# First MLP product by Strassen's seven products, gathered in PSUM; the blocks of both MLP matrices by turns in one buffer

## The chip, the cores and the metric

The kernel runs on one core of a Trainium2 chip. The metric is the device time in microseconds (us) of one execution; lower is better. TensorE multiplies matrices into PSUM, VectorE and ScalarE do elementwise work and read PSUM, GpSimd (POOL) does small elementwise work in SBUF, and SyncE (SP) mostly issues DMA transfers. Each engine works through its own queue in order; between engines there are semaphores.

## The reference

All data are fp32. x is (16, 256, 32, 32): 16 images of 256 channels and S = 1024 pixels. Two layers follow one another:

```python
# layer 0: attention, 4 heads of 64, over the 1024 pixels of an image
qkv = xs @ w_proj + b_proj
res = softmax(q k^T * 64**-0.5) v
x   = res @ w_out + b_out + xs

# layer 1
x = x + attention(group_norm(x), qkv_w, proj_w, proj_b, phys_bias)   # 8 heads of 32
h = group_norm(x)                                                  # 32 groups
h = einsum('oc,bchw->bohw', mlp_w1, h) + mlp_b1                    # 256 -> 1024
h = gelu(h)                                                        # the exact form
h = einsum('oc,bchw->bohw', mlp_w2, h) + mlp_b2                    # 1024 -> 256
return x + h
```

## The kernel before

An image lies in SBUF as 128 partitions x 2 channel blocks x 1024 pixels; the pixels are handled in two blocks of TB = 512. `first_pass` goes through the images in one Python loop, fully unrolled (L1001). Iteration b consists of

- attention 0 of image b (`attention_a`, L354): 32 steps, one for each of 4 (pixel block, channel block) items and 8 blocks of keys. A step makes the scores (L368), their exponential `e` on ScalarE (L376, 8 buffers), the weighing (L389) two steps behind, and on VectorE the running sum of the exponentials `es` (L401), from which the denominators `den` come;
- the first MLP product of image b-1 (`hidden`, L846), 16 pieces, run after attention 0 by `run_pieces` (L1017). In iteration 0 the q, k, v products of image 1 stand here;
- attention 1 of image b (`attention_b`, L478), whose gaps are filled with q, k, v products of the next image's attention 0 and the second MLP product of image b-1 (`reduce`, L886).

Image 15's MLP comes after the loop with no attention beside it (L1066).

**Later work.** `Later` (L31) holds functions with a number of ticks; a tick follows each step of an attention and each piece. The end of attention 0 runs through it beside the MLP pieces: `denominators` (L327) copies the denominators out (L328), spreads them over all partitions by DMA (L333), takes the reciprocal (L337), sends it back through a DRAM row (L338, L343), and `scale` (L440) multiplies the result with it (L446). Four ticks later the projection `out_proj` (L630) runs: products into the two single PSUM banks, then `leave` (L639) adds to x (L641) and takes statistics (L644). The group norm (L668) follows: `means`, three ticks later `variances` (a product `gm` with a 128x128 averaging matrix, then four tiny VectorE operations), one tick later `apply` (a product `gv`, an inverse square root on POOL, the normalised tile by L723). The last denominators of attention 1 are handled in the same way across the border to the next image: they are spread before, and inverted (L337) three steps into attention 0 of the next.

**Order.** A scheduler orders the instructions of each engine by readiness in its own model of the times, so the order need not be the program's. `keep_in_program_order` pins an instruction behind the one traced before it on its engine; the reciprocal L337 and the scaling L446 are pinned so.

**PSUM.** Eight banks of 128 x 512 fp32: three pairs (`wide`, L267), given out with the longest unused first, and two single banks (`bank`).

**The MLP before.** `hidden` makes one 128 x 512 block of the 1024 x 1024 hidden values: two products of 128x128 weights (L849; one for each channel block) into one PSUM bank, then Gelu with bias by ScalarE (L857) to an SBUF tile `g`. The second matrix is multiplied by Strassen's scheme: its seven 4-block sums of quarters lie in `w2s` (made once by POOL, L150), and VectorE makes the sums of the hidden blocks in place by `combine` (L863, L866). w1 lies whole in SBUF as `w1`. Both are loaded once by SP's queue (L164).

Of the kernel before, what the change touches and what calls it, by code (L numbers as in the profile page):

```python
# [8 lines left out]
F32 = mybir.dt.float32  # L9
I32 = mybir.dt.int32  # L10
AF = mybir.ActivationFunctionType
# [3 lines left out]
P = 128  # L15
# [4 lines left out]
TB = 512  # L20
# [34 lines left out]
def kernel(  # L55
# [21 lines left out]
    nc = tc.nc  # L77
    B, C, S = x.shape
    HID = mlp_w1T.shape[1]
    CC = C // P  # L80
# [51 lines left out]
    wo = load_mat(w_out, "wo")  # L132
    wq = load_mat(qkv_wT, "wq")
    wpj = load_mat(proj_wT, "wpj")
    w1 = load_mat(mlp_w1T, "w1")

    w2s = const.tile([P, 7, HID // P // 2, P], F32, name="w2s")

    def quarter(co, half):
        n = HID // P // 2
        return mlp_w2T.rearrange("(c p) n -> p c n", p=P)[
            :, half * n : (half + 1) * n, co * P : (co + 1) * P
        ]

    for n, q in ((2, (0, 0)), (3, (1, 1)), (4, (0, 1)), (1, (1, 0))):
        weights.append((w2s[:, n], quarter(*q)))

    def sum_quarters():  # L150
        q11, q22 = w2s[:, 2], w2s[:, 3]
        nc.gpsimd.tensor_sub(w2s[:, 5], w2s[:, 1], q11)
        nc.gpsimd.tensor_add(w2s[:, 1], w2s[:, 1], q22)
        nc.gpsimd.tensor_sub(w2s[:, 6], w2s[:, 4], q22)
        nc.gpsimd.tensor_add(w2s[:, 4], w2s[:, 4], q11)
        nc.gpsimd.tensor_add(w2s[:, 0], q11, q22)
        nc.gpsimd.tensor_add(m2b2, m2b, m2b)

    def load_rest():
# [48 lines left out]
    with ExitStack() as first:  # L210
        first_pass(
            first, tc, x, out,
            dict(
                wp=wp, bqk=bqk, pb=pb, bo=bo, g1w=g1w, g1b=g1b, g2w=g2w,
                g2b=g2b, pjb=pjb, m1b=m1b, m2b=m2b, wo=wo, wq=wq, wpj=wpj, w1=w1,
                w2s=w2s, m2b2=m2b2, gavg=gavg, mhalf=mhalf, ones=ones, eones=eones,
                bvo=bvo, at_start=at_start, load_rest=load_rest, exp_bias=exp_bias,
                sum_quarters=sum_quarters,
                in_range=in_range,
            ),  # L220
        )

    good = nc.values_load(in_range[0:1, 0:1], min_val=0, max_val=1)
    with tc.If(good == 0):
        with ExitStack() as again:
            general_pass(
                again, tc, x, out,
                dict(
                    wp=wp, bqk=bqk, pb=pb, bo=bo, g1w=g1w, g1b=g1b, g2w=g2w,
                    g2b=g2b, pjb=pjb, m1b=m1b, m2b=m2b, wo=wo, wq=wq, wpj=wpj, w1=w1,  # L230
                    mlp_w2T=mlp_w2T, gavg=gavg, mhalf=mhalf, b_proj=b_proj,
                ),
            )


def first_pass(ctx, tc, x, out, k):
    nc = tc.nc
    B, C, S = x.shape
    CC, SB, NT = C // P, S // P, S // TB
    HC = k["w1"].shape[2] // P  # L240
    later = Later()

    act = ctx.enter_context(tc.tile_pool(name="act", bufs=1))
# [9 lines left out]
    dram = ctx.enter_context(  # L253
        tc.tile_pool(name="dram", bufs=4, space=bass.MemoryType.DRAM)
    )

# [95 lines left out]
    def attention_a(b, qT, kT, v, project):  # L354
# [85 lines left out]
        def scale(t, full):  # L440
            r = res[:, :, t * TB : (t + 1) * TB]
            halves = [
                y.rearrange(form, c=CC, h=2)
                for y, form in ((r, "p c (h q) -> p c h q"), (full, "p (h c q) -> p c h q"))
            ]
            tc.keep_in_program_order(nc.vector.tensor_mul(halves[0], *halves))  # L446
            if t == NT - 1:
                later.after(4, lambda: project(t, res)())

        cols[0] = 32  # L450
        pending = []
# [213 lines left out]
        return issue  # L665


    def group_norm(key, src, stats, gw, gb, tag, out_tile, wait):  # L668
        st = {}

        def averages(name, src):
            ps = wide(name)
            if cols[0] == P:
                product(ps[:, 0, :CC], k["gavg"], src, start=True, stop=True)
                return [(slice(0, P), ps[:, 0, :CC])]
            halves = [slice(h, h + HALF) for h in range(0, P, HALF)]
            for n, sl in enumerate(halves):
                nc.tensor.matmul(  # L680
                    ps[sl, n, :CC], k["gavg"][sl, sl], src[sl], start=True, stop=True
                )
            return [(sl, ps[sl, n, :CC]) for n, sl in enumerate(halves)]
# [23 lines left out]
        def apply():  # L707
            rstd = small.tile([P, CC], F32, tag="rstd", name=f"rstd_{key}")
            for sl, ps in averages(f"gv_{key}", st["tv"]):
                nc.vector.tensor_scalar(rstd[sl], ps, EPS, None, ALU.add)  # L710
            nc.gpsimd.tensor_tensor(rstd, rstd, k["mhalf"], ALU.pow)
            a = small.tile([P, CC], F32, tag="ga", name=f"ga_{key}")
            nc.vector.tensor_mul(a, rstd, gw)
            ma = small.tile([P, CC], F32, tag="gma", name=f"gma_{key}")
            nc.vector.tensor_mul(ma, st["mean"], a)
            c = small.tile([P, CC], F32, tag="gc", name=f"gc_{key}")
            nc.vector.tensor_sub(c, gb, ma)
            y = act.tile([P, CC, S], F32, tag=tag, name=f"gn_{key}")
            out_tile.append(y)
            for t in range(NT):  # L720
                sl = slice(t * TB, (t + 1) * TB)
                for cc in range(CC):
                    nc.vector.tensor_scalar(  # L723
                        y[:, cc, sl], src[:, cc, sl],
                        a[:, cc : cc + 1], c[:, cc : cc + 1], ALU.mult, ALU.add,
                    )

        means()

# [108 lines left out]

    def mlp(b, xb, hn):
        n4 = HC // 2
        gs = {}

        def hidden(t, hc):  # L846
            ps = wide(f"m1_{b}_{t}_{hc}")[:, 0, :]
            for cc in range(CC):
                nc.tensor.matmul(  # L849
                    ps,  # L850
                    k["w1"][:, cc, hc * P : (hc + 1) * P],
                    hn[0][:, cc, t * TB : (t + 1) * TB],
                    start=(cc == 0),
                    stop=(cc == CC - 1),
                )
            g = work.tile([P, TB], F32, tag="g", name=f"g_{b}_{t}_{hc}", bufs=16)
            nc.scalar.activation(g, ps, AF.Gelu, bias=k["m1b"][:, hc : hc + 1])  # L857
            gs[hc // n4, t, hc % n4] = g
            if hc >= n4:

                combine(*(((0, 1), (1, 1)) if t else ((1, 0), (0, 0))), False, hc - n4)

        def combine(to, what, plus, only=None):  # L863
            for i in range(n4) if only is None else (only,):
# [21 lines left out]
        def reduce(number, right, outs, then):  # L886
            ps = wide(f"m2_{b}_{number}")[:, 0, :]
            for i in range(n4):
                product(
                    ps, k["w2s"][:, number - 1, i], gs[(*right, i)],  # L890
                    start=(i == 0), stop=(i == n4 - 1),
                )
            bias, num = None, 1
# [40 lines left out]
            else:  # L934
                add_up()

        return (
            [lambda t=t, hc=hc: hidden(t, hc) for t in range(NT) for hc in range(HC)],
            [lambda what=what: reduce(*what) for what in products],
        )  # L940


    def run(stage, fill=None):
# [35 lines left out]
        start[1]()  # L979
    run_pieces(start[2:])  # L980
    k["exp_bias"]()
    k["sum_quarters"]()


    def fold_bias():
# [15 lines left out]
    for b in range(B):  # L1001
        if b + 1 < B:
            xs[b + 1] = load_x(b + 1)
        xn = []
        run(
            attention_0(
                b, tiles0, xs[b],
                lambda st, b=b, xn=xn: group_norm(
                    f"g{b}", xs[b], st, k["g1w"], k["g1b"], "res", xn, 3
                ),  # L1010
            )
        )
# [3 lines left out]
            first = first_qk + first_v  # L1016
        run_pieces(first if b == 0 else hidden)  # L1017
        later.flush()
        tiles1, (qk, v) = qkv_1(b, xn[0])
        n = len(qk) // CC  # L1020

# [28 lines left out]
        for m, pieces in enumerate(rest):  # L1050
# [4 lines left out]
                b, tiles1, xs[b],  # L1055
                lambda st, b=b, hn=hn: group_norm(
                    f"h{b}", xs[b], st, k["g2w"], k["g2b"], "q1", hn,
                    3 if b + 1 < B else 1,
                ),
            ),  # L1060
            fill,
        )
        run_pieces(end)
        hidden, outputs = mlp(b, xs[b], hn)
    later.flush()
    run_pieces(hidden + outputs)  # L1066

# [15 lines left out]
def general_pass(ctx, tc, x, out, k):  # L1083
# [1 line left out]
    nc = tc.nc  # L1085
    B, C, S = x.shape
    CC, SB, NT, QT = C // P, S // P, S // TB, TB // P
    HC = k["w1"].shape[2] // P

    act = ctx.enter_context(tc.tile_pool(name="g_act", bufs=1))  # L1090
    work = ctx.enter_context(tc.tile_pool(name="g_work", bufs=2))
# [11 lines left out]
    )  # L1103
    ident = small.tile([P, P], F32, name="g_ident", bufs=1)
    make_identity(nc, ident)
    w2 = act.tile([P, HC, C], F32, tag="w2", name="g_w2")
    nc.gpsimd.dma_start(w2, k["mlp_w2T"].rearrange("(c p) n -> p c n", p=P))
    pbs = small.tile([P, HEADS1], F32, name="pbs", bufs=1)
# [167 lines left out]
    with tc.For_i(0, B, 1) as b:  # L1276
# [38 lines left out]
        for t in range(NT):  # L1315
            g = act.tile([P, HC, TB], F32, tag="g", name=f"gg_{t}")
            for hc in range(HC):
                ps = mm_tile(f"gm1_{t}_{hc}")
                for cc in range(CC):
                    nc.tensor.matmul(  # L1320
                        ps,
                        k["w1"][:, cc, hc * P : (hc + 1) * P],
                        hn[:, cc, t * TB : (t + 1) * TB],
                        start=(cc == 0),
                        stop=(cc == CC - 1),
                    )
                nc.scalar.activation(
                    g[:, hc, :], ps, AF.Gelu, bias=k["m1b"][:, hc : hc + 1]
                )
            out_proj("gm2", w2, HC, lambda kc: g[:, kc, :], k["m2b"], xb, t, None)  # L1330
# [40 lines left out]
```

## Time and profile before

| | |
|---|---|
| Median of three runs | 3709.4 us (3708.19 to 3709.4) |
| The profiled execution | 3707.96 us, span 3706.2 us, clock granted to TensorE 0.999 |
| TensorE, VectorE, ScalarE, POOL busy | 99%, 67%, 56%, 3% of the span |
| One middle image's MLP stage (968.15 to 999.60 us) | 31.45 us: TensorE 31.45, VectorE 14.35, ScalarE 10.54, POOL 1.13 |
| Last image's MLP products (L849) | 3647.24 to 3674.98 us |
| DMA | 77.80 MB, 21 GB/s in the mean |

A line of the timeline gives the start and the length in us, the engine, the line of the kernel, the operation with output and inputs, and how many were merged; brackets give the idle time before it and what ended that. A row of the groups gives busy time and mean nanoseconds of one, then the idle time of the engine before them and what ended it. "PEld" is TensorE's loading of weights, which lies beside its matmuls. An fp32 matmul appears as two records. A wait of an engine that is not the bound costs nothing by itself.

### The profile page before, as it was taken

The numbers are of one execution on the slowest core, as the hardware profiler recorded it, in microseconds if no ns is written. First come the engines' busy times: TensorE is split into PE (matmuls) and PEld (weight loads), VectorE is DVE, ScalarE is ACT, GpSimd is POOL, SyncE is SP. The second block draws the span as 40 slices with busy tenths as digits, with TensorE's granted clock in tenths as the row PEclk, the third lists the DMA queues.
The fourth block names the chain that finished last, engine by engine and source line by source line (L and its number), as shares of the span: only waits on it lengthen the run. The fifth ranks groups of instructions, "written<-read, shape, count | busy, mean of one in ns | idle before, by whom it ended". The sixth has DMA issues, their size and how long they took to land.

```text
span 3706.2 us, 79254 instructions
## 1 busy us (share of the span) xinstructions
PE 3685.2 (99%) x34349; PEld 1319.4 (36%) x34349; DVE 2498.0 (67%) x3150; ACT 2084.0 (56%) x2704; POOL 102.9 (3%) x251
## 2 busy tenths in 40 slices
PE   9999999999999999999999999999999999999999
PEld 4333343333423334333343333433333333333333
DVE  4685757757576675766757667586675867657675
ACT  4665646555465564655646465564655656556472
POOL 1000000000000000000000000000000000000000
PEclk9999999999999999999999999999999999999999
DMA  2000100000001010010000100001010000000000
GB/s 87 12 14 10 33 13 13 31 10 33 13 13 36 4 33 13 19 30 7 30 13 19 30 7 31 13 19 30 8 36 7 22 27 13 30 7 22 16 8 27
DMA packets 63395, 77.80 MB, mean 21 GB/s; under 512 B 35038, under 2 KB 37854, under 8 KB 63038
## 3 DMA queue, kind: packets, MB, share of 16 engines
q1 hardware_dynamic: 60892, 71.85, 6.4%
q8 instruction: 271, 4.44, 0.5%
q14 instruction: 86, 0.70, 0.1%
q10 hardware_dynamic: 1746, 0.40, 0.1%
q0 software_dynamic: 400, 0.41, 0.1%
HBM read 54.28 MB, written 17.56 MB: 19 GB/s over the span
## 4 chain that ended last, share of the span: by engine, by line
PE 94%; DVE 3%; issue 2%; ACT 1%; DMA 1%; ACTq 0%; SPq 0%; POOL 0%; DVEq 0%
PE s_b L502 12%; PE acc_b L554 12%; PE s_a L368 12%; PE m L849 12%; PE acc_a L389 11%; PE m L314 10%; PE qk_a L314 6%; PE qk_b L314 5%; PE o L314 3%; PE v_a L314 3%; PE j L314 3%; PE v_b L314 2%; PE den_b L576 1%; DVE es_b L533 1%; PE den_a L420 1%
## 5 line engine op out<-in xcount | busy, mean ns | idle before, releaser
L517 ACT ACTIVATE e_b<-s_b 128x1024 f32<-128x1024 f32 (+1 forms) x1280 | 982.7, 865 | 151.0 <-PE s_b L502 151.0
L533 DVE TENSOR_TENSOR es_b<-es_b,e_b 128x1024 f32<-128x1024 f32 x768 | 899.5, 1219 | 217.2 <-ACT e_b L517 217.1
L376 ACT ACTIVATE e_a<-s_a 128x1024 f32<-128x1024 f32 x512 | 520.8, 1024 | 360.4 <-PE s_a L368 348.1
L502 PE MATMUL s_b<-q,k 32*64 32x512 f32 x8192 | 527.2, 601 | 9.8 <-DVE v L768 7.1
L368 PE MATMUL s_a<-q,k 64*64 64x512 f32 x4096 | 532.6, 593 | 1.1
L389 PE MATMUL acc_a<-e_a,v 64*64 64x512 f32 x4096 | 528.5, 589 | 0.0
L401 DVE TENSOR_TENSOR es_a<-es_a,e_a 128x1024 f32<-128x1024 f32 x384 | 469.4, 1222 | 75.9 <-ACT e_a L376 60.4
L554 PE MATMUL acc_b<-e_b,v 128*32 128x512 f32 x4096 | 492.1, 598 | 0.0
L849 PE MATMUL m<-gn_h,w 128*128 128x512 f32 x1024 | 452.9, 596 | 0.4 <-DVE gn_h L723 0.4
L314 PE MATMUL m<-g,w2s 128*32 128x512 f32 (+1 forms) x3320 | 404.2, 592 | 0.0
L857 ACT ACTIVATE g<-m,m1b 128x512 f32<-128x512 f32 x256 | 175.9, 687 | 339.3 <-PE m L849 339.3
L866 DVE TENSOR_TENSOR g<-g,g 128x512 f32<-128x512 f32 x320 | 209.3, 686 | 147.7 <-ACT g L857 147.4
L502 PEld LDWEIGHTS s_b<-q,k 32*64 32x64 f32 x8192 | 166.3, 130 | 337.3 <-issue 124.6
L849 PEld LDWEIGHTS m<-gn_h,w 128*128 128x128 f32 x1024 | 191.0, 190 | 236.7 <-issue 235.2
L389 PEld LDWEIGHTS acc_a<-e_a,v 64*64 64x64 f32 x4096 | 161.9, 133 | 277.5 <-issue 235.8
L368 PEld LDWEIGHTS s_a<-q,k 64*64 64x64 f32 x4096 | 152.6, 133 | 278.1 <-issue 207.9
L554 PEld LDWEIGHTS acc_b<-e_b,v 128*32 128x32 f32 x4096 | 108.5, 109 | 357.5 <-ACT e_b L517 194.7
L314 PE MATMUL qk_a<-x,wp 128*32 128x512 f32 (+1 forms) x1856 | 233.7, 592 | 0.4 <-ACT k L747 0.4
L314 PE MATMUL qk_b<-gn_g,wq 128*32 128x512 f32 (+1 forms) x1280 | 234.0, 592 | 0.0
L567 DVE TENSOR_TENSOR res_b<-res_b,acc_b 128x512 f32<-128x512 f32 x192 | 131.8, 687 | 143.7 <-PE acc_b L554 143.7
L314 PEld LDWEIGHTS m<-g,w2s 128*32 128x32 f32 (+1 forms) x3320 | 121.5, 112 | 262.2 <-issue 235.8
L768 DVE TENSOR_TENSOR v<-v_b,eones 128x512 f32<-128x512 f32 x64 | 44.1, 689 | 166.0 <-PE v_b L314 166.0
(131 smaller groups left out, 2371.8 us busy)
## 6 DMA issues: line engine op xcount, KB each, us to landing
d_a<-row_a SPq DMA_DIRECT2D x64, 256.0 KB
rd_b<-row_b SPq DMA_DIRECT2D x252, 64.0 KB
out_dram<-x SPq DMA_DIRECT2D x63, 256.0 KB
x<-in_x_dram SPq DMA_DIRECT2D x30, 512.0 KB
x<-in_x_dram SPq DMA_DIRECT2D x4, 256.0 KB
w<-in_L_conv_mlp_w_dram SPq DMA_DIRECT2D x1, 1024.0 KB
w2s<-in_L_conv_mlp_w_dram SPq DMA_DIRECT2D x4, 256.0 KB
sp_b<-rd_b SPq DMA_DIRECT2D x63, 8.0 KB
```

Of the source, the lines that this page charges most:

```text
L314: nc.tensor.matmul(o[sl], w[:, sl], r, **flags)
L368: nc.tensor.matmul(s[h : h + HALF, g, :], kT[g * D : (g + 1) * D, c, kb * P + h : kb * P + h + HALF], qT[g * D : (g + 1) * D, c, t * TB : ...
L376: nc.scalar.activation(e, s, AF.Exp, scale=float(D) ** -0.5)
L389: nc.tensor.matmul(accs[i][h][g * D : (g + 1) * D, :], v[h * HALF : (h + 1) * HALF, kb, c * 2 + g], e[h * HALF : (h + 1) * HALF, g, :], st ...
L401: nc.vector.tensor_add(sums[i], held[i] if kb == 1 else sums[i], e)
L502: nc.tensor.matmul(outs[g][h : h + HALF, :], kT[g * D : (g + 1) * D, c, k0 : k0 + HALF], qT[g * D : (g + 1) * D, c, t * TB : (t + 1) * TB] ...
L517: nc.scalar.activation(to, s, AF.Exp, scale=float(D) ** -0.5)
L533: ins = nc.vector.tensor_add(d, es[n % 2] if kb == 0 else d, es[n])
L554: nc.tensor.matmul(acc[g * D : (g + 1) * D, :], v[:, kb + m, c * G + g], es[2 * m + g // 2][:, g % 2, :], start=(m == 0), stop=(m == 1),)
L849: nc.tensor.matmul(ps, k["w1"][:, cc, hc * P : (hc + 1) * P], hn[0][:, cc, t * TB : (t + 1) * TB], start=(cc == 0), stop=(cc == CC - 1),)
L857: nc.scalar.activation(g, ps, AF.Gelu, bias=k["m1b"][:, hc : hc + 1])
L866: (nc.vector.tensor_add if plus else nc.vector.tensor_sub)(d, d, gs[(*what, i)])
```

## The change

The first MLP product also goes by seven products instead of eight. The quarters of w1 (128 channels x 512 hidden values) and the 2 x 2 blocks of the normalised input (128 channels x 512 pixels) take the places of Strassen's scheme. `make_blocks` forms seven blocks of either matrix on POOL in the first iteration and stores them in DRAM (`kept_blocks`). One SBUF buffer of 14 KB per partition (tag "ws") then holds by turns w1's blocks (loaded at the head of attention 0) and w2's (loaded after the MLP pieces); for image 15 the w1 blocks are loaded into two other tiles. The general pass, which runs only where denominators are out of range, loads w1 itself.

`sums_of_input` makes the five input sums on VectorE after the second group norm, three of them into a new tile "hs", one per tick. The hidden pieces become 12 for each image: `begin`, `middle` and `finish` for each of four blocks i, in pairs. `begin` makes products 2, 5 and 1; ScalarE copies product 2 negated out of PSUM, and VectorE forms the fourth quadrant's share. `middle` adds products 4 and 3 onto products 2 and 5 in the same banks, which gives two quadrants. `finish` adds products 7 and 6 to the same banks, which VectorE adds to the kept share for the other two quadrants. Three other places change: the projection of attention 0 comes 3 ticks after scaling instead of 4, the group norm's variances come 2 ticks after the means instead of 3 (both from image 1 on), and its averages use a single bank where whole 128-column products run.

```diff
+    def make_blocks(m, t, keep):
+        q = quarters(m)
+        for n, ij in ((2, (0, 0)), (3, (1, 1)), (4, (0, 1)), (1, (1, 0))):
+            to = t[:, n]
+            nc.gpsimd.dma_start(
+                to if m == 1 else to.rearrange("p (c n) -> p c n", n=P), q(*ij)
+            )
+        q11, q22 = t[:, 2], t[:, 3]
+        nc.gpsimd.tensor_sub(t[:, 5], t[:, 1], q11)
+        nc.gpsimd.tensor_add(t[:, 1], t[:, 1], q22)
+        nc.gpsimd.tensor_sub(t[:, 6], t[:, 4], q22)
+        nc.gpsimd.tensor_add(t[:, 4], t[:, 4], q11)
+        nc.gpsimd.tensor_add(t[:, 0], q11, q22)
+        nc.gpsimd.dma_start(keep, t)
...
+    def load_blocks(m, b, at_end=False):
+        if not at_end:
+            t = act.tile([P, 7, TB], F32, tag="ws", name=f"w{m}_{b}")
+            nc.sync.dma_start(t, kept_blocks[m])
+            blocks[m] = [t[:, n] for n in range(7)]
+            return
+        one = act.tile([P, 4, TB], F32, tag="k0", name=f"w{m}_{b}_0")
+        two = act.tile([P, 4, TB], F32, tag="x", name=f"w{m}_{b}_1", bufs=3)
+        nc.sync.dma_start(one, kept_blocks[m][:, :4])
+        nc.sync.dma_start(two[:, :3], kept_blocks[m][:, 4:])
...
-                later.after(4, lambda: project(t, res)())
+                later.after(3 if b else 4, lambda: project(t, res)())
...
+            if cols[0] == P:
+                ps = bank(name, 1)
+                product(ps[:, :CC], k["gavg"], src, start=True, stop=True)
+                return [(slice(0, P), ps[:, :CC])]
             ps = wide(name)
...
+    def sums_of_input(b, y):
+        extra = act.tile([P, 3, TB], F32, tag="hs", name=f"hs_{b}")
+        y11, y12 = (y[:, 0, t * TB : (t + 1) * TB] for t in range(NT))
+        y21, y22 = (y[:, 1, t * TB : (t + 1) * TB] for t in range(NT))
+        s1, s6, s7 = (extra[:, n] for n in range(3))
+        inputs[b] = {1: s1, 2: y11, 3: y12, 4: y21, 5: y22, 6: s6, 7: s7}
+        todo = [
+            lambda: nc.vector.tensor_add(s1, y11, y22),
+            lambda: nc.vector.tensor_add(s7, y21, y22),
+            lambda: nc.vector.tensor_sub(y21, y21, y11),
+            lambda: nc.vector.tensor_add(s6, y11, y12),
+            lambda: nc.vector.tensor_sub(y12, y12, y22),
+        ]
+        for n, fn in enumerate(todo):
+            if b < B - 1:
+                later.after(1 + n, fn)
+            else:
+                fn()
...
+        def products_of(i, to):
+            for number, ps, first in to:
                 nc.tensor.matmul(
+                    ps, blocks[1][number - 1][:, i * P : (i + 1) * P],
+                    inputs[b][number], start=first, stop=True, skip_group_check=not first,
+                )
...
+        def begin(i):
+            ps = wide(f"m1_{b}_{i}")
+            if i % 2 == 0:
+                open_sums["once"] = wide(f"m1_{b}_{i}_1")
+            once = open_sums["once"][:, i % 2, :]
+            open_sums[i] = ps
+            products_of(i, [(2, ps[:, 0, :], True), (5, ps[:, 1, :], True), (1, once, True)])
+            minus, rest = unit(0, 1, i), unit(1, 1, i)
+            nc.scalar.activation(minus, ps[:, 0, :], AF.Copy, scale=-1.0)
+            nc.vector.tensor_sub(rest, minus, ps[:, 1, :])
+            nc.vector.tensor_add(rest, rest, once)
+
+        def middle(i):
+            ps = open_sums[i]
+            products_of(i, [(4, ps[:, 0, :], False), (3, ps[:, 1, :], False)])
+            unit(1, 0, i)
+            gelu(1, 0, i, ps[:, 0, :])
+            gelu(0, 1, i, ps[:, 1, :])
+
+        def finish(i):
+            ps = open_sums.pop(i)
+            products_of(i, [(7, ps[:, 0, :], False), (6, ps[:, 1, :], False)])
+            rest = gs[1, 1, i]
+            nc.vector.tensor_add(unit(0, 0, i), rest, ps[:, 0, :])
+            nc.vector.tensor_add(rest, rest, ps[:, 1, :])
+            gelu(0, 0, i, gs[0, 0, i])
+            gelu(1, 1, i, rest)
+            combine((1, 0), (0, 0), False, i)
+            combine((0, 1), (1, 1), False, i)
+
+        hidden = [
+            lambda part=part, i=i: part(i)
+            for i0 in range(0, n4, 2) for part in (begin, middle, finish) for i in (i0, i0 + 1)
+        ]
...
-    k["sum_quarters"]()
+    for m in (1, 2):
+        made = act.tile([P, 7, TB], F32, tag="ws", name=f"w{m}_made")
+        k["make_blocks"](m, made, kept_blocks[m])
+    nc.gpsimd.tensor_add(k["m2b2"], k["m2b"], k["m2b"])
...
+        if b:
+            load_blocks(1, b - 1)
         run(
             attention_0(
                 b, tiles0, xs[b],
                 lambda st, b=b, xn=xn: group_norm(
-                    f"g{b}", xs[b], st, k["g1w"], k["g1b"], "res", xn, 3
+                    f"g{b}", xs[b], st, k["g1w"], k["g1b"], "res", xn, 2 if b else 3
                 ),
             )
         )
...
         later.flush()
+        if b:
+            load_blocks(2, b - 1)
+        if b == B - 1:
+            load_blocks(1, b, True)
```

## The prediction

> **What bounds the kernel now.** I read the page's busy times first, then the chain, then the MLP rows, then the timeline of one middle image engine by engine (us 955 to 1010), and last the waits at the head of attention 0. From the page:
>
> ```profile
> PE 3685.2 (99%) x34349; PEld 1319.4 (36%) x34349; DVE 2498.0 (67%) x3150; ACT 2084.0 (56%) x2704; POOL 102.9 (3%) x251
> ...
> PE 94%; DVE 3%; issue 2%; ACT 1%; DMA 1%; ACTq 0%; SPq 0%; POOL 0%; DVEq 0%
> ...
> L849 PE MATMUL m<-gn_h,w 128*128 128x512 f32 x1024 | 452.9, 596 | 0.4 <-DVE gn_h L723 0.4
> ...
> L857 ACT ACTIVATE g<-m,m1b 128x512 f32<-128x512 f32 x256 | 175.9, 687 | 339.3 <-PE m L849 339.3
> L866 DVE TENSOR_TENSOR g<-g,g 128x512 f32<-128x512 f32 x320 | 209.3, 686 | 147.7 <-ACT g L857 147.4
> ```
>
> TensorE is the bound (94% of the chain), so what counts is how much matmul time goes, and whether any new wait stops TensorE. L849 is the matrix the change touches; 1024 records are 512 products (two records each). The chain of waits gives the true pace, and the VectorE timeline shows who stands at the head of its queue there:
>
> ```profile
> 968.15 10.50 PE m L849 x24
> 978.65 3.43 PE o L314 x8
> 982.08 5.15 PE m L849 x12
> ```
>
> ```profile
> 954.18 0.69 DVE L406 TENSOR_TENSOR res_a<-res_a,acc_a 128x512 f32<-128x512 f32 x1
> 954.78 1.22 DVE L446 TENSOR_TENSOR res_a<-res_a,d_a 128x1024 f32<-128x1024 f32 x1
> 955.92 7.87 DVE L401 TENSOR_TENSOR es_a<-es_a,e_a 128x1024 f32<-128x1024 f32 x6
> 964.40 0.69 DVE L406 TENSOR_TENSOR res_a<-res_a,acc_a 128x512 f32<-128x512 f32 x1 [0.61 <-ACT res_a L405]
> ...
> 969.61 0.23 DVE L337 RECIPROCAL inv_a<-sp_a 128x16 f32<-128x16 f32 x1
> 975.94 1.23 DVE L446 TENSOR_TENSOR res_a<-res_a,d_a 128x1024 f32<-128x1024 f32 x1 [6.09 <-DMA d_a<-row_a]
> ```
>
> 12 records in 5.15 us are 6 products, so 0.858 us each with no gap. VectorE waits 6.09 us for a transfer inside the MLP stage, while TensorE does not notice. VectorE runs without a pause before the stage (six adds, L401) and has little room there. Finally the DMA side, at the head of attention 0:
>
> ```profile
> 902.08 0.81 SPq L292 DMA_DIRECT2D x<-in_x_dram  x2
> 904.21 0.54 SPq L333 DMA_DIRECT2D sp_b<-rd_b  x1
> ```
>
> ```profile
> 907.07 0.25 DVE L337 RECIPROCAL inv_b<-sp_b 128x16 f32<-128x16 f32 x1 [5.40 <-DMA sp_b<-rd_b]
> ```
>
> The small sp_b transfer stands behind 1.05 MB of x, and VectorE waits for it.
>
> [...]sp_b takes 2.86 us to VectorE behind x, against 2.0 for sp_a alone (issue at 967.15, the POOL add that waits for it at 969.15).
>
> **The change, part by part.** Fifteen MLP stages lie between two attentions (images 0 to 14), one at the end (image 15).
>
> 1. *Products.* 32 per image become 28: 4 x 0.858 = 3.43 us saved per image, 54.9 in all. Weight loads go with them. Each of the 28 loads its own 128x128 weights as before (190 ns, L849 on PEld, beside the matmuls).
>
> 2. *Five input sums per image* (SBUF, 128x512, VectorE), one per step in the last third of attention 0. Start to start such an add costs 0.60 us (954.18 to 954.78), five cost 3.0. The cover is thin: six adds at 1.15 (954.78 to 955.92) would bring the last one to 961.67, and it runs at about 962.5 because its exponential ends at 962.23. So 0.8 is hidden, and 2.2 delays it, to about 964.7, and the L406 add behind it to 965.85 to 966.54, instead of ending at 965.09. TensorE's denominators (den_a) use the PSUM pair that this L406 reads, and now start at 965.39. Stall about 966.55 - 965.39 = 1.15 us per image. Bounds: 0 if the scheduler puts the sums behind the adds, 1.8 if each costs its full 0.69.
>
> 3. *The MLP stage*, from t=0 at its first matmul. The pieces go begin, begin, middle, middle, finish, finish (2.57, 2.57, then 1.72 each), twice. Per image 8 adds in begin, 8 in finish, 4 negating copies on ScalarE (0.58 us, taken from L405, also a copy out of PSUM); VectorE 16 x 0.69 = 11.0 us more in a stage of about 29 (14.35 of 31.45 by the windows now).
>  The reciprocal (L337) is pinned behind what was traced before it on VectorE. That is now the second add of the first begin, which waits for the third product: 2.57+0.23, ends at 3.49. It now runs at 1.46. So it is about 2.0 us later, and its row and broadcast transfers with it: 3.7+6.1 = 9.8, scale (L446) to 11.05. The projection is now issued after five pieces, 10.29 (3 ticks instead of 4). Stall about 0.8 us. Bounds 0 (transfer as quick as a microsecond less) and 1.8 (7.04 us, as once in the trace).
>  Behind scale in VectorE's queue: finish's two adds (to 12.4), two combines that wait for gelus (to 13.9), the projection's two stt and statistics (to about 17.2), the second finish's adds (to 18.5). The second pair's first begin needs the PSUM pair freed at 12.4 and comes at 16.3; the second begin needs the pair freed at 18.5 and comes at 18.96: no stall, 0.4 to spare. The variances' four small operations stand behind begin's adds (21.3), end at 22.1; TensorE wants gv at 21.5: stall 0.6, or 0 if they slip ahead; I take 0.3. The normalised tile is written by 26, TensorE needs it at about 29: hidden. Late gelus and combines at the end fall under the 8.6 us of qk and v products that follow.
>  The gelu table load (1.28 us) keeps its number, and lies beside begin. The averages' move from a wide pair to one bank costs nothing, since the leave before it has read that bank.
>  Sum per middle image: 3.43 - 1.15 - 0.8 - 0.3 = 1.2 us; times 15 = 18.
>
> 4. *Weights by turns.* 7 x 2 KB x 128 = 1.84 MB, loaded twice per image by SP's queue. w2's load is issued when the last MLP product has read the buffer; its first user came 41 us after that (999.5 to 1040.4), and 1.84 MB at the 352 to 385 GB/s of the x load takes 5.1 us: hidden. w1's load joins x at the head of attention 0, and what is queued behind it is sp_b, then the pinned reciprocal, then all of VectorE's adds. 2.89 MB from about 903 end at 911, so the reciprocal runs at about 912 instead of 907.1. TensorE stalls only when ScalarE's ninth exponential (916.60) finds no free one of its 8 buffers. The first add, 1.2 us after the reciprocal, frees two. So up to about 915.2 it costs nothing, and VectorE catches up at 1.15 per 1.72 us step. I take 0; bounds 0 and 4 us per image.
>
> 5. *Start.* Two weight loads move from SP to POOL, with ten POOL sums (1.26 us each now, five of them there before) and two stores. POOL's next user that matters is the first group norm (110.8). At an estimated 60 us, worked out from these and the load rate, it is done. Zero.
>
> 6. *Tail.* Saved 3.43; product 5 needs y22, the last of four writes, about 0.5 us late, and product 1 its sum, 0.6 more. w1 for it comes early into other tiles, and w2 is still there from the image before. No attention work competes, and the PSUM pairs come free in time (0.6 us to spare by the same steps). Net 2.3.
>
> Sum: 18 + 2.3 = about 20 us. The profiled execution took 3707.96 us (span 3706.2), so 3688. The median of the runs shown is 3709.4, 0.04% above it. I forecast 3688, 0.5 to 0.6% less.
>
> **Rivals.** A measurement here tells changes above 0.2% (7.4 us) from none.
> *All hidden.* The scheduler places the sums and small operations so that no stall comes: 54.9 less the tail's 1.1 gives 3654. For it: TensorE has hidden a 6.09 us wait of VectorE. Against: the pin and the full VectorE before den_a.
> *No net.* Stalls of about 3.4 per image eat the gain: part 3 with its upper bounds, 1.8+1.15+0.6. About 3706. For it: four tight places in one stage. Against: each has its own slack.
> *Slower, by the block load.* Transfers at half the rate (180 GB/s, 5 us more) put the reciprocal at 917; with x held behind out's landing (SP waits there already, 24.6 us in 13 times) at 919, 4 us beyond 915.2. Then 15 x (4 - 1.2) - 2 = 40 us more than before: 3748. It decides from about 916.5, where the stall equals the 1.2 us gained. For it: 5.40 us of wait at this place already. Against: the measured 352 to 385 GB/s leaves 3 us to spare.
> *Slower, by VectorE's queue.* If it runs 3 us later than worked out at the second begin (a leave ahead of a finish, a combine waiting for a gelu queued behind a copy), the PSUM pair is late by 2.6 and gv adds little: 15 x (2.6 - 1.2) - 2 = 19 more, 3727. For it: VectorE is busy 14.35 of the stage's 31.45 us now, and 25 of 29 then. Against: after scale it has no other long wait.
>
> **How the numbers follow.** Forecast 0.45 (own range 3672 to 3701); all hidden 0.12 (3648 to 3664); no net 0.13 (3701 to 3716); block load 0.12 (3717 to 3760); VectorE's queue 0.18 (3717 to 3745). Faster is the first two, 0.57; same 0.13; slower 0.30. The range 3664 to 3732 leaves out most of the second (0.1) and the upper part of the last two (about 0.1).
>
> **What would show it.** Right: 896 records instead of 1024 at 0.858 us a product; den_a waiting about 1 us for L406; the projection waiting under 1 us for scale; recip inv_b at about 912, with ScalarE not waiting for it. Wrong: matmuls that accumulate in PSUM at another pace; TensorE waiting at s_a for buffers near 917; waits of over 1 us at the second begins; or w2's load not landed at its first product.

## The result, and the profile after

The changed kernel takes 3700.46 us (median of 11 runs, 3698.11 to 3701.68), the kernel before 3708.99 on the same chip (11 runs, 3707.29 to 3709.69): ratio 0.9977, 95% interval 0.9967 to 0.9986. It is faster by 0.23%; 0.5 to 0.6% was forecast. The profiled execution took 3700.63 us (span 3698.8; before 3707.96 and 3706.2).

The page of the kernel after: its first line, its chain, and the two rows of TensorE's products with the first matrix (m is the product, gn_h the normalised input, hs the sums in the new tile):

```profile
PE 3644.9 (99%) x34221; PEld 1290.8 (35%) x34221; DVE 2688.2 (73%) x3486; ACT 2118.4 (57%) x2768; POOL 121.1 (3%) x266
...
PE 81%; DVE 14%; issue 3%; DMA 1%; ACT 1%; POOL 1%; SPq 0%; DVEq 0%; ACTq 0%
...
L898 PE MATMUL m<-gn_h,w 128*128 128x512 f32 x512 | 243.7, 604 | 5.7 <-DVE g L924 3.3
...
L898 PE MATMUL m<-hs,w 128*128 128x512 f32 x384 | 177.9, 592 | 0.1
```

The products went down as meant: 512 + 384 = 896 records against 1024, and TensorE's busy time fell by 40.3 us. The span fell by 7.4. The chain shows that something stands between the two: VectorE held 3% of the chain before and holds 14% now. The waits of TensorE name the place (us in total, times, longest):

```profile
PE den_a L442 <- DVE res_a L428: 28.1, 15, 1.9
```

Fifteen times TensorE waits 1.9 us to begin the denominators of attention 0. This row did not exist before. Below, an image is counted by the attention 0 that runs; the MLP beside its end is that of the image before. The chain of image 4, as it stands in time, shows what TensorE waits through (start, length, then engine, tile and line):

```profile
952.99 0.60 DVE hs L878
953.59 0.60 DVE hs L875
954.19 0.60 DVE hs L876
954.79 0.07 DVE gn_h L879
...
964.21 1.24 DVE es_a L423
...
965.54 1.23 DVE es_a L423
966.77 0.61 DVE res_a L428
967.38 0.04 issue
967.42 1.07 PE den_a L442 x16
968.49 1.72 PE o L336 x16
970.21 13.09 PE m L898 x30
```

From 953 to 967.4 the end is set by VectorE, with only short pauses for issue: the input sums (L875 to L879), then the running sums of exponentials (L423), then the addition to the result (L428), for which den_a waits. In the kernel before, TensorE stood in the chain at this place. A table by stage, read from TensorE's timeline, gives images 1 to 15 at once (us). The stages begin with the first scores of attention 0 (s_a), the first projection products at its end (o), the first MLP product (m), the first q and k products of attention 1 (qk_b), and its first scores (s_b). The images agree to 0.1, except where the table or the text says otherwise:

| | attention 0 | its end, with den_a | MLP stage | to attention 1 | attention 1 |
|---|---|---|---|---|---|
| before | 60.22 | 4.43 | 31.45 (image 1: 31.98) | 8.69 | 124.34 |
| after | 60.22 | 6.52 | 28.72 (image 2: 30.39) | 8.79 | 124.34 |

So an image gains 2.73 in the MLP stage, and gives back 2.08 (unrounded) at den_a and 0.10 at its exit: 0.55 net instead of the 1.2 forecast. Fifteen times that is 8.3 us. The way from there to the 7.4 measured, by subtraction of the two timelines: image 2 costs 1.7 more, one stretch of slow clock 1.7 (last section), the start 0.5; the end of the program gives 2.3, the last image 0.1, and two delays of the kernel before that are absent now give 0.5 (the MLP stage of image 1) and 0.2 (attention 1 of image 7). That sums to 7.5, which leaves 0.1 for rounding.

Image 2 is no accident of one execution: its stage is longer than the others by 0.9 to 2.0 us in every profiled run below that has the seven products. A slow transfer makes it so (see step 3 below); what slows that, no run shows.

### The profile page after: what moved, and what is told of

It is laid out like the page before. It is cut to its first block, busy times and chain, and to the rows that moved or that the text cites. A ratio compares the mean times of both kernels' runs of the same rounds, so it can differ in the third digit from the quotient of the medians.

```text
span 3698.8 us, 79399 instructions
## 1 busy us (share of the span) xinstructions
PE 3644.9 (99%) x34221; PEld 1290.8 (35%) x34221; DVE 2688.2 (73%) x3486; ACT 2118.4 (57%) x2768; POOL 121.1 (3%) x266
## 4 chain that ended last, share of the span: by engine, by line
PE 81%; DVE 14%; issue 3%; DMA 1%; ACT 1%; POOL 1%; SPq 0%; DVEq 0%; ACTq 0%
PE s_b L524 12%; PE acc_b L576 12%; PE m L336 10%; PE s_a L390 9%; PE acc_a L411 8%; PE m L898 6%; PE qk_a L336 6%; PE qk_b L336 5%; DVE es_a L423 4%; PE v_a L336 3%; PE j L336 3%; PE v_b L336 2%; PE den_b L598 1%; DVE g L954 1%; DVE es_b L555 1%
## 5 line engine op out<-in xcount | busy, mean ns | idle before, releaser
L423 DVE TENSOR_TENSOR es_a<-es_a,e_a 128x1024 f32<-128x1024 f32 x384 | 471.0, 1226 | 58.4 <-ACT e_a L398 39.1
L576 PE MATMUL acc_b<-e_b,v 128*32 128x512 f32 x4096 | 493.8, 600 | 0.0
L336 PE MATMUL m<-g,w 128*32 128x512 f32 (+1 forms) x3320 | 404.3, 592 | 0.0
L898 PE MATMUL m<-gn_h,w 128*128 128x512 f32 x512 | 243.7, 604 | 5.7 <-DVE g L924 3.3
L576 PEld LDWEIGHTS acc_b<-e_b,v 128*32 128x32 f32 x4096 | 108.6, 109 | 358.2 <-ACT e_b L539 194.8
L336 PEld LDWEIGHTS m<-g,w 128*32 128x32 f32 (+1 forms) x3320 | 121.4, 112 | 262.3 <-issue 235.0
L898 PE MATMUL m<-hs,w 128*128 128x512 f32 x384 | 177.9, 592 | 0.1
L555 DVE TENSOR_TENSOR es_b<-e_b,e_b 128x1024 f32<-128x1024 f32 x128 | 150.6, 1217 | 0.0
L911 ACT ACTIVATE g<-g,m1b 128x512 f32<-128x512 f32 x128 | 92.1, 722 | 99.6 <-DVE g L938 72.7
```

What stands on the lines that cost most here:

```text
L336: nc.tensor.matmul(o[sl], w[:, sl], r, **flags)
L423: nc.vector.tensor_add(sums[i], held[i] if kb == 1 else sums[i], e)
L555: ins = nc.vector.tensor_add(d, es[n % 2] if kb == 0 else d, es[n])
L576: nc.tensor.matmul(acc[g * D : (g + 1) * D, :], v[:, kb + m, c * G + g], es[2 * m + g // 2][:, g % 2, :], start=(m == 0), stop=(m == 1),)
L898: nc.tensor.matmul(ps, blocks[1][number - 1][:, i * P : (i + 1) * P], inputs[b][number], start=first, stop=True, skip_group_check=not first,)
```

## The experiments

Theory A: the sums' place in VectorE's queue, ahead of the last running sums of attention 0, costs most of their length (2.08 of 3.0 us), and nothing else of the change costs much. Rivals: the MLP stage itself is short of VectorE (then sums put elsewhere come back as a stall there); the transfers of weight blocks cost; the seven-product form has a loss of its own at the ends.

**The sums taken out.** The products read blocks of the input that are not summed:

```diff
-        inputs[b] = {1: s1, 2: y11, 3: y12, 4: y21, 5: y22, 6: s6, 7: s7}
-        todo = [
-            lambda: nc.vector.tensor_add(s1, y11, y22),
...
-        for n, fn in enumerate(todo):
...
+        inputs[b] = {1: y11, 2: y11, 3: y12, 4: y21, 5: y22, 6: y12, 7: y21}
```

> The changed kernel without the five input sums; the products take unsummed blocks in their place, so the output is another. Theory A (the sums on VectorE hold back the last running sums of the exponentials, and den_a with them): the gap from the first projection products to the first MLP product falls from 6.51 us to the 4.43 of before in each of 15 images, 31 us, and the tail loses its wait too (about 2.5): 3667 us. Theory B (the lost gain lies in the MLP stage itself, in PSUM pairs and VectorE's queue there): that gap shrinks but the stage grows by as much, 3695 to 3700. Theory C (the block loads delay attention): no change, 3700.

Measured: 3667.2 us (4 runs, 3666.52 to 3668.02), ratio 0.989 (0.9873 to 0.9906). The end of attention 0 is back at 4.43, and the MLP stage stays at 28.72. All of the 2.08 is the sums', and the MLP stage does not grow when the stall ahead of it goes.

**The same sums' worth of work in the kernel before**, as maxima of a block with itself, which alter nothing:

```diff
+            if then:
+                then(y)
...
+        todo = [
+            lambda p=p: nc.vector.tensor_tensor(p, p, p, ALU.max)
+            for p in (*parts, parts[0])
+        ]
+        for n, fn in enumerate(todo):
+            if b < B - 1:
+                later.after(1 + n, fn)
...
```

> The kernel before with five more 128x512 VectorE operations (maximum of a block of the normalised tile with itself) at the places of the sums, nothing else changed. Theory A: den_a comes 2.08 us later in each of 15 images, 31 us more: 3740. Theories B and C: hidden, 3709 to 3712.

Measured: 3738.95 us (4 runs, 3738.3 to 3740.97), ratio 1.0083 (1.0066 to 1.01). The end of attention 0 takes 6.52, exactly as in the kernel after, with the MLP stage at its old 31.45. Added to the kernel before, the five operations cost 31.6 us (it takes 3707.37 on that chip); taken from the changed one, they give back about 32 by the two ratios, the tail's 2.1 among them. The stall needs no other part of the change.

**The sums on POOL**, which is idle 97% of the time, for all images but the last:

```diff
+        eng = nc.gpsimd if b < B - 1 else nc.vector
         todo = [
-            lambda: nc.vector.tensor_add(s1, y11, y22),
...
+            lambda: eng.tensor_add(s1, y11, y22),
...
```

> The changed kernel with the five sums on POOL for images 0 to 14. Theory A: POOL takes 1.26 us an add alone, up to 2.3 beside VectorE (start of the changed kernel), so five are done in 6 to 11 us after the normalised tile, before the 17 us that pass until the MLP stage; den_a's wait goes: 15 x 2.08 = 31 us less, 3669. Rival: POOL and VectorE slow each other in SBUF, so that VectorE's adds lose as much as they are spared: 3695 or more. Theories B and C: 3695 to 3700.

Measured: 3730.91 us (4 runs, 3729.8 to 3732.44), ratio 1.0063 (1.0046 to 1.0079), slower than both kernels. The rival stated with the expectation (POOL and VectorE slow each other) held; the 3669 that theory A gave missed by over 60 us. POOL's timeline and, at the same moments, VectorE's (start, length, idle time before in brackets):

```profile
962.05 2.26 POOL L876 TENSOR_TENSOR hs<-gn_h 128x512 f32<-128x512 f32 x1
...
964.28 2.25 POOL L877 TENSOR_TENSOR hs<-gn_h 128x512 f32<-128x512 f32 x1
...
966.50 2.25 POOL L880 TENSOR_TENSOR gn_h<-gn_h 128x512 f32<-128x512 f32 x1
...
968.71 2.25 POOL L878 TENSOR_TENSOR gn_h<-gn_h 128x512 f32<-128x512 f32 x1
```

```profile
963.10 11.60 DVE L423 TENSOR_TENSOR es_a<-es_a,e_a 128x1024 f32<-128x1024 f32 x6
974.62 0.68 DVE L428 TENSOR_TENSOR res_a<-res_a,acc_a 128x512 f32<-128x512 f32 x1
```

A POOL addition that takes 1.26 us alone (at the start of the kernel before) takes 2.25 here, and six running sums take 11.60 instead of 7.87. Both engines are slowed while both add in SBUF: VectorE's running sums around this place, of 1.22 us in the kernel after, have a median of 2.11, close to POOL's 2.25. How the two hold each other up, no run here shows. den_a then waits 2.99 us instead of 1.87, and L428 still stands behind it all. The rest of the loss is in the clock, granted at 0.996 in the mean (kernel after: 0.999): TensorE ran at half its clock in nine stretches of 3.41 us, each one begun right behind this wait, which is about 15 us where the change's own execution lost 1.7. The products that stand there show it: those of den_a and the first projection products take 36.3 and 74.2 us in all, where the kernel after has 34.2 and 61.2. With 15 times 1.12 us more at den_a that covers the 30 us between the two executions.

**The last image's sums spread out.** The last image's five sums were issued at once; here the first is, and the others at two per tick:

```diff
+elif n:
+    later.after((n + 1) // 2, fn)
 else:
     fn()
```

> The changed kernel with the last image's sums spread over the first pieces (one at once, two after the first, two after the second) as the products need them. If the tail's lost gain is VectorE's queue (five sums ahead of the add that frees a PSUM pair, 1.34 us of wait, and the third product behind the sums), the time from the first MLP product to the second matrix falls from 27.44 by about 2 us. If it is the PSUM pairs as such: unchanged.

Measured: 3699.44 us (one run, span 3697.7, against 3698.8). From the last image's first product to the second matrix takes 26.33 us, after 27.44, before 27.57. So 1.1 of the expected 2 comes, which in one run of the total can't be told from nothing; the stage shows it. The scheduler still put the five sums side by side in VectorE's order. What moved is the addition to x for which TensorE had waited 1.34 us: it now runs ahead of the sums (L1011, at 3643.39) instead of behind them (L1009, at 3646.41), and a wait of 0.56 for another addition takes the place of the 1.34. Without any sums (the first experiment) the same stretch takes 25.36.

**The sums after the end of attention 0.** Only the first sum stays in attention 0; the other four are pinned in program order behind the first projection block's leave. The last image as in the run above:

```diff
+if b < B - 1 and n:
+    late_sums.append(lambda fn=fn: tc.keep_in_program_order(fn()))
+elif n:
+    later.after((n + 1) // 2, fn)
 # in attention_a, after the first half of the last item
+while late_sums:
+    late_sums.pop(0)()
```

> The changed kernel with only the first of the five sums left in attention 0; the other four are pinned in VectorE's order behind the statistics of the first projection block, that is behind the add that den_a waits for (and the tail's sums spread as in the run before). Theory A: den_a is held back by one add, 0.60 us of which 0.3 are covered, so the gap to the MLP stage falls from 6.51 to about 4.7; the four sums take 2.4 us between that and the first begin's adds, the reciprocal comes up to 1 us later, and the projection, which now comes 12.9 us into the stage, still does not wait. About 15 x 1.8 + 1.1 = 28 us less than the changed kernel: 3671. Rival (VectorE is so full from the end of attention 0 through the MLP stage that work moved only moves the stall): the gap shrinks and the stage grows from 28.72 by as much, 3695 to 3700.

Measured: 3666.84 us (4 runs, 3665.86 to 3668.2), ratio 0.9887 (0.987 to 0.9903): faster than the kernel before by 1.1% and than the change by 0.9%, 4 us better than expected. It leaves out nothing of the reference. The end of attention 0 takes 4.43, the MLP stage 28.72 (image 2: 29.95). TensorE's and VectorE's timelines of image 4:

```profile
956.53 1.92 PE L336 MATMUL o<-res_a,wo 128*32 128x512 f32 x16
...
958.27 1.05 PE L442 MATMUL den_a<-es_a,ones 128*32 128x256 f32 x16
...
959.13 1.90 PE L336 MATMUL o<-res_a,wo 128*32 128x512 f32 x16
...
960.97 1.98 PE L902 MATMUL m<-gn_h,w 128*128 128x512 f32 x4
```

```profile
957.32 0.68 DVE L428 TENSOR_TENSOR res_a<-res_a,acc_a 128x512 f32<-128x512 f32 x1
958.52 0.75 DVE L665 SCALAR_TENSOR_TENSOR x<-o,bvo,x 128x512 f32<-128x512 f32 x1 [0.52 <-PE o L336]
...
959.92 0.68 DVE L878 TENSOR_TENSOR hs<-gn_h 128x512 f32<-128x512 f32 x1
...
965.08 0.25 DVE L359 RECIPROCAL inv_a<-sp_a 128x16 f32<-128x16 f32 x1
...
971.40 1.22 DVE L468 TENSOR_TENSOR res_a<-res_a,d_a 128x1024 f32<-128x1024 f32 x1 [3.73 <-DMA d_a<-row_a]
```

L428 runs with no sum but one ahead of it, and den_a starts without a bracket: the one sum fits into the 0.61 us that L428 waited for ScalarE in the kernel before. The other four (the first of them at 959.92) fill time that VectorE later spent waiting: it still waits 3.73 us for a transfer before L468. That answers the rival on the MLP stage: 2.4 us more of VectorE's work there (four sums at 0.60) cost nothing.

**The combining subtractions behind both finishing additions of a pair**, in addition to the edit above, to see whether they delay the PSUM pairs:

```diff
-combine((1, 0), (0, 0), False, i)
-combine((0, 1), (1, 1), False, i)
+if i % 2:
+    for j in (i - 1, i):
+        combine((1, 0), (0, 0), False, j)
+        combine((0, 1), (1, 1), False, j)
```

> The same, and the in-place combines of a pair of blocks are issued after both blocks' finishing adds, so that the adds which free a PSUM pair do not queue behind combines that wait for Gelu. The changed kernel's own waits for that are 0.2 us a middle image at the second pair and 0.57 in the tail. If these are the adds' place in the queue: 3 to 4 us less than the run before; if it is ScalarE's Gelu that is late: no difference.

Measured: 3665.9 us (4 runs, 3665.7 to 3668.17), ratio 0.9886 (0.987 to 0.9903). That isn't told apart from 3666.84, and the wait that it aimed at stays, in TensorE's timeline of the last image, then VectorE's:

```profile
3625.36 2.84 PE L902 MATMUL m<-gn_h,w 128*128 128x512 f32 x6 [0.57 <-DVE g L943]
```

```profile
3624.02 0.69 DVE L960 TENSOR_TENSOR g<-g,g 128x512 f32<-128x512 f32 x1
3624.62 0.68 DVE L943 TENSOR_TENSOR g<-g,m 128x512 f32<-128x512 f32 x1
```

The same 0.57 stands in the run before. But L943, the addition that TensorE waits for, runs behind two combining subtractions (the second is the L960 shown) here as there: the scheduler kept VectorE's order at this place, whatever the order in the program. So this run does not test whether their place causes the wait, and that stays open. In the middle images one subtraction did move back; the MLP stage then takes 28.81 us instead of 28.72.

**The second matrix's blocks not loaded**; the first's stand in for them:

```diff
-if b:
-    load_blocks(2, b - 1)
+blocks[2] = blocks.get(1)
```

> The changed kernel without the loads of the second matrix's blocks: the first's stand in their place (another output), so 1.84 MB per image and the wait for the buffer fall away. Theory A: nothing changes, 3699 to 3700. Theory C (the turns in one buffer delay attention 0 or the second product): up to 15 x 1 us less, 3685.

Measured: 3703.29 us (one run, span 3701.5), no less than the 3700.46 with the loads. The stages equal those of the change to 0.1 us, but for two images in which den_a waits 2.23 and 2.25 us instead of 1.87. The excess of 2.7 us in span is these waits and the clock: two half-clock stretches, behind waits of 1.22 us (143.24) and 2.23 us (1426.80), where the change's execution has one. So these loads, 1.84 MB per image, cost nothing that can be seen where they lie. The first matrix's loads were not taken out; that they cost attention 0 nothing is read from its 60.22 us in both kernels.

**The test of denominators moved ahead of the last MLP, in the kernel before.** The change's program ends 4.0 us after VectorE's last addition to x, the kernel before 6.3 us after it, though nothing in the change was meant to do so. In the trace of the kernel before, the test of the denominators' range stands behind that addition; in the trace of the changed kernel it is done 45 us ahead of it. Moving the block alone:

```diff
     later.flush()
-    run_pieces(hidden + outputs)
...
     ok = small.tile([P, 2], F32, name="ok", bufs=1)
...
     nc.vector.tensor_copy(k["in_range"][0:1], both[0:1])
+    run_pieces(hidden + outputs)
```

> The kernel before with the last test of the denominators' sums (one product and a few tiny operations) traced ahead of the last image's MLP instead of behind it. In the changed kernel this test ran 50 us before the end, and the stretch from VectorE's last instruction to the span's end fell from 6.3 to 4.0 us. If the test's place is the cause and not the new MLP, this one gains the same 2.3: span about 3704.

Measured: 3704.95 us (one run, span 3703.1, against 3706.2). VectorE's last addition ends at 3699.14, and the span 4.0 later, as in the kernel after (3694.82 to 3698.8). So these 2.3 us come from the order in which the end of the program is issued, not from the products. The single total lies 2.1 us below the lowest run of the kernel before on this chip (3707.05).

## Why the prediction was wrong in size

The mechanism was right: the products go, the stage shortens, and sums ahead of L428 stall den_a. The sign was right, and VectorE's queue at that very place was named. What failed is the size of a term.

**Step 2, the five sums: mis-sized, and it decides.** It gave a stall of 1.15 us per image, because six additions "at 1.15" from 955.92 left 0.8 us of slack. Measured is 2.08, so 0.93 more; fifteen times that is 14 us, which is more than the whole miss (12.5 us between 3688 and 3700.5). VectorE's timeline of the kernel after:

```profile
954.71 0.68 DVE L879 TENSOR_TENSOR gn_h<-gn_h 128x512 f32<-128x512 f32 x1
955.32 0.68 DVE L877 TENSOR_TENSOR gn_h<-gn_h 128x512 f32<-128x512 f32 x1
955.92 1.22 DVE L423 TENSOR_TENSOR es_a<-e_a,e_a 128x1024 f32<-128x1024 f32 x1
957.16 0.69 DVE L428 TENSOR_TENSOR res_a<-res_a,acc_a 128x512 f32<-128x512 f32 x1
957.77 1.22 DVE L468 TENSOR_TENSOR res_a<-res_a,d_a 128x1024 f32<-128x1024 f32 x1
958.90 7.87 DVE L423 TENSOR_TENSOR es_a<-es_a,e_a 128x1024 f32<-128x1024 f32 x6
966.69 0.68 DVE L428 TENSOR_TENSOR res_a<-res_a,acc_a 128x512 f32<-128x512 f32 x1
```

The pace of 1.14 was taken from L446 (now L468) to the add behind it, which do not depend on each other. The six running sums each take the one before as input, and the chain above shows them at 964.21 and 965.54: 1.33 us apart. They last 7.87 us here, behind 3 us of other work, and they lasted the same 7.87 in the kernel before, where they also start 1.33 apart. So they were never held up by the exponentials; the row shown with the prediction, "7.87 ... x6", already said 1.31 each. That the dependence makes the pace is seen beside it: attention 1 of the kernel before adds by turns into two sums, and there three of the same shape take 3.49, 1.14 from start to start:

```profile
1062.81 3.49 DVE L533 TENSOR_TENSOR es_b<-es_b,e_b 128x1024 f32<-128x1024 f32 x3
```

So the slack of 0.8 was a misreading. Without it, L428 moved by 2.29 (964.40 to 966.69) and den_a by 2.03 in this image. The upper bound given, 1.8 (1.6 by its own terms), was too low for the same reason. What remains of the 3.0 is hidden: L428 had waited 0.61 for its copy from ScalarE before, and no longer does, and den_a had begun 0.30 after the end of that addition (L406 there).

**Step 3, the stage.** Forecast 3.43 - 0.8 - 0.3 = 2.33 saved; measured 2.73. The 0.8 at the projection did not come, because the scheduler put it later than its tick. TensorE's timeline, then VectorE's:

```profile
978.83 4.46 PE L898 MATMUL m<-hs,w 128*128 128x512 f32 x10
983.12 3.60 PE L336 MATMUL o<-res_a,wo 128*128 128x512 f32 x8
986.55 3.60 PE L898 MATMUL m<-gn_h,w 128*128 128x512 f32 x8
```

```profile
974.19 0.25 DVE L359 RECIPROCAL inv_a<-sp_a 128x16 f32<-128x16 f32 x1
...
980.75 1.23 DVE L468 TENSOR_TENSOR res_a<-res_a,d_a 128x1024 f32<-128x1024 f32 x1 [3.91 <-DMA d_a<-row_a]
```

The scaling ends at 981.98, inside the first stretch, so the projection at 983.12 finds its input. The scaling at t = 10.6 to 11.8 (t = 0 at 970.14) is near the forecast 9.8 to 11.05. Only in image 2 was the transfer 1.83 us longer (3.26 against 1.43 from the issue of the row's store to that of its load), and there TensorE waited 0.53 us for the scaling and later 1.03 at the second pair. Matmuls that go on accumulating after other engines have read the bank keep their pace: 10 records in 4.29 us, 0.858 per product. That was a bare assumption before.

Two small waits took the place of the one expected, both at a weight load (PEld) that waits for VectorE to have read PSUM:

```profile
990.31 0.30 PEld L898 LDWEIGHTS m<-gn_h,w 128*128 128x128 f32 x2 [0.99 <-DVE g L924]
...
998.85 0.30 PEld L336 LDWEIGHTS qk_b<-gn_g,wq 128*128 128x128 f32 x2 [0.94 <-DVE g L939]
```

Counted on TensorE they are about 0.3 each: eight records from 986.55 end at 989.98, and eight from 995.15 at 998.58. The forecast had 0.3 for one such wait, at gv, and none at the exit, where late work was said to be covered. The second begins were right: no stall.

**Step 4, the blocks by turns.** The cost of zero was right, by another route than reasoned. SP's timeline and VectorE's at the head of attention 0:

```profile
899.23 0.34 SPq L270 DMA_DIRECT2D w<-w_kept  x1
...
904.20 0.54 SPq L355 DMA_DIRECT2D sp_b<-rd_b  x1
...
907.72 0.82 SPq L314 DMA_DIRECT2D x<-in_x_dram  x2
```

```profile
906.79 0.25 DVE L359 RECIPROCAL inv_b<-sp_b 128x16 f32<-128x16 f32 x1 [5.15 <-DMA sp_b<-rd_b]
```

The blocks go first, and x stands behind sp_b instead of ahead of it. The reciprocal therefore runs at 906.79, near the 907.07 of before, not at about 912. The rival "slower, by the block load" needed it beyond 915.2.

**Steps 5 and 6.** The start cost 0.5 us, not zero. The last image gave 0.13 us instead of 2.3: two waits stand in TensorE's timeline of the tail, the first for an addition to x that runs behind the five sums:

```profile
3647.21 1.98 PE L898 MATMUL m<-gn_h,w 128*128 128x512 f32 x4 [1.34 <-DVE x L1009]
...
3660.11 2.84 PE L898 MATMUL m<-gn_h,w 128*128 128x512 f32 x6 [0.57 <-DVE g L939]
```

1.34 and 0.57 us of it are waits within the stage; the edit that spreads the sums in the program returned 1.1, leaving them out 2.1. The end's 2.3 us, in no step, made up for it by chance, and only with them does 3700.46 lie within the forecast's own range (3672 to 3701).

**The rivals.** "No net" (3706) described the outcome's kind best: stalls eat most of the gain. (Its three terms sum to 3.55, not to 3.4, which would make it some 2 us more.) But it put them at four tight places, and the one at den_a alone ate three quarters of the 2.73 gained in the stage. "All hidden" (3654) is not what this kernel does; with the sums moved it comes to 3666.84, within 13 us of it.

## What to carry to other kernels

Before you count slack on an engine's queue, divide the row you have by its count: a chain in which each operation reads the result of the one before can run slower than independent operations of the same shape (here one every 1.33 us instead of every 1.14), and a queue that looks held up by another engine may simply be full. Work added to an engine that isn't the bound can cost most of its length where that engine's last result releases the bound (here 2.08 of 3.0 us), and nothing a few microseconds later where the engine waits for a transfer (here four sums, with the MLP stage unchanged at 28.72 us), so choose the place from the engine's waits and pin it. An idle engine is no free place for the work if the two slow each other in SBUF, as POOL and VectorE did here (an addition of POOL 2.25 us instead of 1.26, VectorE's 2.11 instead of 1.22).

## What the runs showed that was not expected

A running sum of 128x1024 fp32 (L423) starts 1.33 us after the one it depends on; independent additions of the same shape (L533 of the kernel before) follow at 1.14 (each lasts 1.22).

TensorE's clock falls to half in single stretches of 3.41 us in at least six of the ten profiled executions (the end of the program, where TensorE has no more work, left aside). In the kernel after one lies behind a wait of 1.22 us at 3542.11, in its timeline and in the window from 3543 to 3547 (the last columns: granted clock, share of DMA, GB/s):

```profile
3542.11 1.09 PE L524 MATMUL s_b<-q,k 32*64 32x512 f32 x8 [1.22 <-DVE v L793]
3543.13 3.57 PE L576 MATMUL acc_b<-e_b,v 128*32 128x512 f32 x16
```

```profile
3543.00:3547.00 4.00, 4.00 (x25) 1.01 (x25) 0.44 (x2) 1.02 (x1) 0.00 (x0) 0.57 0.00 0
```

The kernel before has the same wait of 1.22 us at this place, and its 16 products behind it take 1.92 us instead of 3.57. In the kernel after the granted clock is 0.50 from 3543.4 to 3546.6 and 1.00 again from 3546.7. Such a stretch costs 1.7 us, half its length. Two of the other runs have one behind the same wait (the last image's sums spread out, and the sums after the end of attention 0: the 16 products take 3.32 and 3.45 us), and the run without the second matrix's blocks has one behind the wait of 1.22 us in image 0 (3.28 us). Without the sums all products of that kind (L576) take 493.6 us, as in the kernel after (493.8), and 492.1 in the kernel before. In the run with the sums on POOL nine stand behind the waits of 2.96 to 2.99 us at den_a, while six waits of that length have none; the fifteen waits of up to 1.9 us at den_a in the kernel after have none either. So the length of the wait alone doesn't decide it. Why one wait does and an equal one doesn't, no run tells.
